# Layer 1 of a two-layer expert kernel: pinned residual additions and weightings, and tiles turned ahead of the products

## Chip, cores and metric

The kernel runs on one core of a Trainium2 chip. The metric is the device time of one execution in microseconds (us). Before the change it is 2111.94 us, the median of three runs. The core has five engines that run side by side, each in its own instruction order: PE (TensorE, the matrix array), DVE (VectorE), ACT (ScalarE), POOL (GpSimd) and SP (SyncE, which only issues transfers here). They wait for each other through semaphores.

## What is computed

A network of two layers on an input of 4 sequences of 512 rows with 512 columns, all in float32. Each layer computes `x = x + attention(layernorm(x)) + experts(layernorm(x))`. The change lies in layer 1, whose two parts are, cut to what matters:

```python
# attention: 16 heads of 32 columns
scores = jnp.einsum('bhqd,bhkd->bhqk', q, k) * scale
attn = jax.nn.softmax(scores, axis=-1)
ctx = jnp.einsum('bhqk,bhkd->bhqd', attn, v)
out = ctx @ wo_w.T + wo_b

# experts: 8 experts, the best 2 for each row
h = jnp.einsum('td,edf->etf', xf, expert_w) + expert_b[:, None, :]
expert_out = jax.nn.silu(h)
combined = jnp.einsum('etf,te->tf', expert_out, full_w.reshape(-1, E))
y = x + combined @ proj_w + proj_b
rms = jnp.sqrt(jnp.mean(y * y, axis=-1, keepdims=True) + EPS)
return norm_w * (y / rms)
```

## The kernel before

Layer 0 fills the time to about 1480 us and is not touched. Layer 1 has 2048 rows, 16 row tiles of 128 rows. Its attention is done in 16 groups g (4 sequences times 4 sets of 4 heads), and each group in 4 places kc, one for each 128 keys. At every place (g, kc) the program records, in this order: the scores of the 4 heads (`weights`, tile `st`, L1114, one matmul a head on a quarter of the array's rows, and the exponential on ACT, L1116, into `pT`), the product with the values of the place before (`attend`, tile `cx`, L1128, with additions on DVE into `pS`, L1134), at some places the key sums (`sum_keys`, `sm`, L1142), inverses (L1152) and scaling of the context (L1160), the next group's queries (`qp`, L1090, with DVE steps L1095 to L1105), the next sequence's values (`vp`, L1050) or a finished tile of the attention's output (`output1`, `o`, L1197). Then `run1((g, kc))` runs the expert jobs that are listed for this place.

These jobs are a list `jobs1` of pairs (place, function); at one place they run in the order of the list. The expert work has two stages.

In the expert stage the rows of x, sorted by expert, are handled in 39 tiles of 128 rows. `fetch_rows`, `fetch_weights` and `fetch_bias` gather a tile's rows, weights and bias by indirect transfers that POOL issues (L384). `turn(i)` transposes the tile on PE (`trm`, L409), and ACT copies the result to `xT` (L411, one buffer). `apply(i)` multiplies (`hp`, L419), adds the bias on DVE into `yr` (L421), takes a tanh on ACT (L425), finishes on DVE (L426) and writes the tile to memory (L427). Tile i is applied at `here = first + 4 + i * 11 // 13`, so about every sixth or seventh place holds two tiles.

In the mixing stage `mix(n)` gathers the two expert results of each row of row tile n (`row0`, `row1`, L434, POOL), loads the tile of normalised x (`xa`, L1222, SP), weights and adds the two results on DVE (L1225, L1226), and adds a bias row on POOL (L1227). One place later `turn_mix` transposes (`trc`, L1234; ACT copy L1238) and brings the partly summed residual tile (`bring`, L1182, SP). `project_mix` multiplies with the projection (`po`, L1245), adds it to `xa` (DVE, L1246), squares and sums on ACT (`ysq`, L1249), and POOL forms the inverse root (`yss`, L1250 and L1251). `finish_mix` scales `xa` by it (DVE, L1256) and calls `add_part`.

`add_part` (L1186) adds one of the two parts, attention or experts, to the residual tile. The second of the two additions is followed by the store to the output (L1189), the first by a store to a scratch array `accd` (L1191) where the tile has to wait in memory. SP issues these stores and loads in its own order.

PSUM holds three banks for the tag "mm", which `hp`, `trm`, `qp`, `vp`, `sm`, `o`, `trc` and `po` take in turn, two double banks for `st` and one for `cx`.

The order of each engine's instructions is not the recorded one: a scheduler in the tile framework reorders them by its own estimates. An instruction that is wrapped in `tc.keep_in_program_order(...)` keeps the place that the program gives it on its engine.

Of the kernel before, what the change touches and what calls it, by code (L numbers as in the profile page):

```python
# [15 lines left out]
ALU = mybir.AluOpType  # L16
# [14 lines left out]
NS = 2 * T // P + E - 1  # L31
# [13 lines left out]
def two_layers(ctx: ExitStack, tc: tile.TileContext, a: dict, out: bass.AP, large: bass.AP):  # L45
# [3 lines left out]
    V, G, A, PE = nc.vector, nc.gpsimd, nc.scalar, nc.tensor  # L49
# [468 lines left out]
    rout = {}  # L518
# [238 lines left out]
    def second_logits(b, pool, bank):  # L757
        def get(rows_):
            V.tensor_tensor(lg1[:, ts(b, TC), :], rows_, rout["rb"].unsqueeze(1).to_broadcast([P, TC, E]), ALU.add)
        return logits(b, rout["rw"], pool, "r1", get, bank)[1]  # L760
# [8 lines left out]
    for b in range(1, B):  # L769
        i = b - 2  # L770
# [46 lines left out]
    at = [(i, h) for i in range(5, len(steps)) for h in range(4)]  # L817
# [5 lines left out]
    at = [(i, h) for i in range(5, len(steps)) for h in (0, 2, 4) if (i, h) > at[2 * NS - 1]]  # L823
# [24 lines left out]
    for n in range(3 * TC):  # L848
        i, t = 29 + n // TC, n % TC
# [13 lines left out]
    qkT, sums_x, first, second, third, fourth, fifth, turn_queries, turn_keys = project(0)  # L863
# [49 lines left out]
    for i, (g, b) in enumerate(steps):  # L913
# [11 lines left out]
        if more:  # L925
            load_sums(i + 1)
            qkT, sums_x, first, second, third, fourth, fifth, turn_queries, turn_keys = project(i + 1)
# [255 lines left out]

    def add_part(n, part_, way):
        x = lies.pop((n, way))
        V.tensor_tensor(x, x, part_, ALU.add)  # L1186
        left[n] -= 1
        if left[n] == 0:
            nc.sync.dma_start(out=out_v[n], in_=x)  # L1189
        elif (n, 1 - way) not in lies:  # L1190
            nc.sync.dma_start(out=accd[ts(n, P), :], in_=x)  # L1191

    def output1(b, t):
        n = b * TC + t
        op = bank1("mm", f"o1_{n}")
        for jj in range(NJ):
            PE.matmul(op, lhsT=cT1[b][:, jj, ts(t, P)], rhs=wa["woT"][:, jj, :],  # L1197
                      start=(jj == 0), stop=(jj == NJ - 1))
        add_part(n, op, 0)

    r1 = Routing("r1", lg1, rp, const, bank1)
# [16 lines left out]
    def mix(n):  # L1218

        g0, g1 = rout["ex1"].gather(n)  # L1220
        x = rout["mix"].tile([P, HID], F32, tag="xr", name=f"xa_{n}")
        nc.sync.dma_start(out=x, in_=xnd[ts(n, P), :])  # L1222

        pin = tc.keep_in_program_order if n < 2 else (lambda x: x)
        pin(V.tensor_scalar(g0, g0, r1.gate[:, 0, n : n + 1], None, ALU.mult))  # L1225
        V.scalar_tensor_tensor(g0, g1, r1.gate[:, 1, n : n + 1], g0, ALU.mult, ALU.add)  # L1226
        G.tensor_tensor(x, x, rows["pb"], ALU.add)  # L1227
        held[n] = g0, x
# [25 lines left out]
    def finish_mix(n):  # L1254
        y, ss = held.pop(n)
        V.scalar_tensor_tensor(y, y, ss[:, 0:1], rows["nw1"], ALU.mult, ALU.mult)  # L1256
        add_part(n, y, 1)


    at = [(g, kc) for g in range(NG) for kc in range(TC)]  # L1260
    jobs1 = [(at[0], lambda: second_logits(B - 1, rp, bank1)()), (at[1], r1.choose), (at[3], r1.place)]
# [5 lines left out]
    first = 9  # L1267
# [3 lines left out]
        jobs1.append((at[first], lambda i=i: rout["ex1"].fetch_weights(i)))  # L1271
        jobs1.append((at[first], lambda i=i: rout["ex1"].fetch_bias(i)))
    jobs1.append((at[first], lambda: rout["ex1"].fetch_weights(2)))
    for i in range(NS):

        here = first + 4 + i * 11 // 13
        jobs1.append((at[here - 1], lambda i=i: rout["ex1"].turn(i)))
        jobs1.append((at[here - 1], lambda i=i: rout["ex1"].fetch_rows(i + 2)))
        jobs1.append((at[here], lambda i=i: rout["ex1"].apply(i)))
        jobs1.append((at[here], lambda i=i: rout["ex1"].fetch_weights(i + 3)))  # L1280
        jobs1.append((at[here], lambda i=i: rout["ex1"].fetch_bias(i + 2)))
    first += 6 + NS * 11 // 13
    jobs1.append((at[first], begin_mixing))
    for n in range(NT):
        here = first + n * 13 // 16
        for d, f in ((0, mix), (1, turn_mix), (2, project_mix), (3, finish_mix)):
            jobs1.append((at[here + d], lambda n=n, f=f: f(n)))
# [78 lines left out]
    for t in range(TC):  # L1366
        PE.matmul(last[t], lhsT=cT1[B - 1][:, NJ - 1, ts(t, P)], rhs=wa["woT"][:, NJ - 1, :], start=False, stop=True)
        add_part(n0 + t, last[t], 0)
        if t == 0:
            fine = bank1("mm", "fine")  # L1370
            PE.matmul(fine[0:1, 0:1], lhsT=ends[:, 0, 0:1], rhs=ones[:, 0:1], start=True, stop=True)
            few = small.tile([1, 1], F32, tag="few", name="few")
            V.tensor_scalar(few, fine[0:1, 0:1], P - 0.5, None, ALU.is_lt)
            V.tensor_tensor(large, few, wide, ALU.max)
# [686 lines left out]
```

## Time and profile before

| what | value |
|---|---|
| time, median of 3 runs | 2111.94 us (2111.6 to 2112.5) |
| the profiled execution | 2114.76 us |
| its span | 2112.8 us |
| mean granted TensorE clock | 0.996 |
| busy: PE, DVE, ACT, POOL | 2057.1, 1463.7, 872.0, 732.8 us |
| L419, the products of the expert tiles, both layers | 520 matmuls, 235.0 us |
| waits of DVE at L1256 (`xa`) for POOL at L1251 (`yss`) | 29.7 us in 14 times |
| layer 1's expert stage | from the first transposes at 1583.84 us to about 1945 us |
| layer 1's mixing stage | about 1948 to 2091 us |

The span is the time between the first and the last instruction in the trace; the time of an execution is a little longer. Times of single instructions come from one profiled execution and are counted from the start of its span. A row of the timeline gives the start, the duration, the engine, the line, the operation, its output and inputs, and how many like instructions it stands for; a bracket behind it tells how long the engine was idle before it and which instruction ended that. Matmuls overlap at their ends, so differences of starts are used for what a group takes.

### The profile page before, as it was taken

How to read it: one execution, taken by the hardware profiler on the slowest of the kernel's cores; microseconds unless marked ns; L12 is line 12 of the kernel's file. 1: busy time of each engine (PE TensorE's matmuls, PEld its weight loads, DVE VectorE, ACT ScalarE, POOL GpSimd, SP SyncE). 2: the span in 40 equal slices, each digit the busy share in tenths (PEclk: the TensorE clock that was granted, in tenths of full speed). 3: DMA queues.
4: the chain of work that ended last, by engine and by line, in shares of the span. 5: the costliest groups of instructions: out<-in, count | busy, mean ns of one | idle time of the engine just before them, and what ended most of it. 6: DMA issues, size and time to landing. Idle time of an engine off the chain costs nothing.

```text
span 2112.8 us, 27908 instructions
## 1 busy us (share of the span) xinstructions
PE 2057.1 (97%) x9138; PEld 1229.1 (58%) x9138; DVE 1463.7 (69%) x3514; ACT 872.0 (41%) x2661; POOL 732.8 (35%) x722
## 2 busy tenths in 40 slices
PE   7999999999999999999999999999999999999988
PEld 4566666666666666666666666665334445445443
DVE  7978967666766766666676778787486555556775
ACT  3444544444444444444443444444243332333332
POOL 3322244443323333333332344453113432332650
PEclk9999999999999999999999999999999999999999
DMA  7201123323332333343233222221316775673551
GB/s 251 76 31 58 39 97 114 143 100 110 126 127 95 121 136 100 110 141 111 95 134 129 76 70 71 70 90 61 115 57 220 258 239 181 217 239 122 143 167 56
DMA packets 95818, 258.73 MB, mean 122 GB/s; under 512 B 12913, under 2 KB 25201, under 8 KB 85681
## 3 DMA queue, kind: packets, MB, share of 16 engines
q0 software_dynamic: 25712, 139.48, 20.0%
q1 hardware_dynamic: 68800, 115.29, 16.4%
q10 hardware_dynamic: 1152, 2.10, 0.3%
q8 instruction: 75, 1.23, 0.2%
q14 instruction: 79, 0.64, 0.1%
HBM read 212.52 MB, written 44.30 MB: 122 GB/s over the span
## 4 chain that ended last, share of the span: by engine, by line
PE 78%; DVE 9%; issue 4%; ACT 4%; POOL 3%; DMA 2%; SPq 0%; ACTq 0%; POOLq 0%; DVEq 0%
PE p L555 22%; PE hp_r L419 13%; PE op L722 10%; PE st L647 4%; PE qp L1090 3%; PE st L1114 3%; PE sp L638 2%; PE cx L1128 2%; PE trm_r L409 2%; PE o L1197 2%; ACT sq L459 2%; PE ca L691 2%; PE vp L1050 1%; PE trq L575 1%; PE trs L673 1%
## 5 line engine op out<-in xcount | busy, mean ns | idle before, releaser
L722 PE MATMUL op<-Wo,cT 128*128 128x512 f32 x512 | 230.4, 598 | 4.9 <-DVE lv L619 3.1
L419 PE MATMUL hp_r<-we_r,xT_r 128*128 128x512 f32 x520 | 235.0, 595 | 0.0
L655 POOL TENSOR_TENSOR lT<-lT,lmask 128x512 f32<-128x512 f32 (+1 forms) x128 | 156.4, 1234 | 182.5 <-ACT lT L651 182.3
L384 POOL DMA_INDIRECT xr_r<-xnd,rows_r x78 | 101.1, 1296 | 293.0 <-PE trm_r L409 243.9
L555 PE MATMUL p<-wB,x 128*128 128x384 f32 x512 | 176.4, 488 | 4.1 <-DVE u L611 3.4
L555 PE MATMUL p<-wT,x 128*128 128x384 f32 x512 | 179.5, 493 | 0.7 <-DVE wT L106 0.7
L555 PE MATMUL p<-wA,xnT 128*128 128x384 f32 x512 | 173.3, 489 | 0.4 <-DVE u L590 0.4
L722 PEld LDWEIGHTS op<-Wo,cT 128*128 128x128 f32 x512 | 92.0, 190 | 114.6 <-issue 77.2
L459 ACT ACTIVATE sq<-qb 128x128 f32<-128x128 f32 x384 | 119.0, 310 | 89.9 <-DVE qb L604 35.3
L419 PEld LDWEIGHTS hp_r<-we_r,xT_r 128*128 128x128 f32 x520 | 94.8, 190 | 104.5 <-issue 96.0
L1116 ACT ACTIVATE pT<-st 128x1024 f32<-128x1024 f32 x128 | 123.9, 1018 | 68.4 <-PE st L1114 57.4
L725 DVE TENSOR_TENSOR acc<-acc,op 128x512 f32<-128x512 f32 x128 | 87.7, 685 | 72.3 <-PE op L722 72.0
L555 PEld LDWEIGHTS p<-wB,x 128*128 128x128 f32 x512 | 94.0, 190 | 67.5 <-issue 9.6
L555 PEld LDWEIGHTS p<-wT,x 128*128 128x128 f32 x512 | 95.2, 193 | 63.3 <-issue 8.9
L555 PEld LDWEIGHTS p<-wA,xnT 128*128 128x128 f32 x512 | 95.0, 192 | 59.8 <-DVE u L590 1.6
L411 ACT COPY xT_r<-trm_r 128x512 f32<-128x512 f32 x78 | 45.3, 581 | 203.4 <-PE trm_r L409 168.0
L569 ACT ACTIVATE qb<-qb,ss 128x128 f32<-128x128 f32 x256 | 81.9, 390 | 111.6 <-POOL ss L461 108.5
L651 ACT ACTIVATE lT<-st,ss 128x256 f32<-128x256 f32 (+1 forms) x128 | 46.8, 448 | 177.8 <-PE st L647 177.7
L647 PE MATMUL st<-qkT 128*128 128x256 f32 (+1 forms) x512 | 109.3, 354 | 0.0
L434 POOL DMA_INDIRECT row_r<-yd,slot_r x64 | 74.8, 1169 | 96.2 <-DVE row_r L1226 35.5
L647 PEld LDWEIGHTS st<-qkT 128*128 128x128 f32 x512 | 92.0, 191 | 10.9 <-issue 1.0
L461 POOL TENSOR_TENSOR ss<-ss,nhalf 128x6 f32<-128x6 f32 x64 | 95.2, 1488 | 5.3
(320 smaller groups left out, 4334.3 us busy)
## 6 DMA issues: line engine op xcount, KB each, us to landing
x<-xsd SPq DMA_DIRECT2D x112, 256.0 KB
yd<-yr_r SPq DMA_DIRECT2D x78, 256.0 KB
wA<-in_wA SPq DMA_DIRECT2D x16, 384.0 KB
wB<-in_wB SPq DMA_DIRECT2D x16, 384.0 KB
xnd<-xn SPq DMA_DIRECT2D x24, 256.0 KB
accd<-acc SPq DMA_DIRECT2D x18, 256.0 KB
acc<-in_x SPq DMA_DIRECT2D x16, 256.0 KB
Wo<-in_Wo SPq DMA_DIRECT2D x8, 512.0 KB
```

Source lines behind the costliest of these rows:

```text
L384: G.indirect_dma_start(out=out, out_offset=None, in_=src, in_offset=at_rows(idx[:, i : i + 1]))
L419: PE.matmul(hp, lhsT=xT[:, k, :], rhs=w[:, ts(k, HID)], start=(k == 0), stop=(k == KC - 1))
L434: G.indirect_dma_start(out=x, out_offset=None, in_=self.yd, in_offset=at_rows(self.r.slot[:, k, n : n + 1]))
L459: A.activation(sq, x[:, h, :], AF.Square, accum_out=ss[:, h : h + 1])
L461: G.tensor_tensor(ss, ss, nhalf[:, 0:n], ALU.pow)
L555: PE.matmul(p, lhsT=x[:, k, ts(c, P)], rhs=w[:, k, :], start=(k == 0), stop=(k == 1))
L569: A.activation(x[:, j, :], x[:, j, :], AF.Copy, scale=sq[t][:, j : j + 1])
L647: PE.matmul(st[:, ds((t % 2) * 256, n)], lhsT=qkT[:, HG + h, ts(t, P)], rhs=qkT[:, h, ds(t * P, n)], start=True, stop=True)
L655: G.tensor_tensor(dst, dst, lmask.rearrange("p a w j -> p (a w j)")[:, 0:n], ALU.mult)
L722: PE.matmul(op, lhsT=cT[:, h, ts(t, P)], rhs=wo[:, h, :], start=(h == 0), stop=(h == HG - 1))
L725: V.tensor_tensor(acc[:, n, :], acc[:, n, :], op, ALU.add)
L1116: A.activation(pt[:, ts(pair, 2), :], st, AF.Exp, scale=SCALE1)
```

## The change

Three edits. The addition in `add_part` is kept in program order for all tiles. The first of the two weightings in `mix` is kept in program order for all row tiles, where it was so for the first two. In the expert stage the jobs for turning a tile and for fetching the rows of the next but one now stand in the list ahead of all products, so at one place they run before them; and of two tiles that are applied at the same place, only the first is turned one place earlier, the second at that place itself.

```diff
     def add_part(n, part_, way):
         x = lies.pop((n, way))
-        V.tensor_tensor(x, x, part_, ALU.add)
+        tc.keep_in_program_order(V.tensor_tensor(x, x, part_, ALU.add))
         left[n] -= 1
...
-        pin = tc.keep_in_program_order if n < 2 else (lambda x: x)
-        pin(V.tensor_scalar(g0, g0, r1.gate[:, 0, n : n + 1], None, ALU.mult))
+        tc.keep_in_program_order(V.tensor_scalar(g0, g0, r1.gate[:, 0, n : n + 1], None, ALU.mult))
         V.scalar_tensor_tensor(g0, g1, r1.gate[:, 1, n : n + 1], g0, ALU.mult, ALU.add)
...
-    for i in range(NS):
-
-        here = first + 4 + i * 11 // 13
-        jobs1.append((at[here - 1], lambda i=i: rout["ex1"].turn(i)))
-        jobs1.append((at[here - 1], lambda i=i: rout["ex1"].fetch_rows(i + 2)))
+
+    here_ = [first + 4 + i * 11 // 13 for i in range(NS)]
+    turned_at = [h - (i == 0 or here_[i - 1] < h) for i, h in enumerate(here_)]
+    for i, h in enumerate(turned_at):
+        jobs1.append((at[h], lambda i=i: rout["ex1"].turn(i)))
+        jobs1.append((at[h], lambda i=i: rout["ex1"].fetch_rows(i + 2)))
+    for i, here in enumerate(here_):
         jobs1.append((at[here], lambda i=i: rout["ex1"].apply(i)))
         jobs1.append((at[here], lambda i=i: rout["ex1"].fetch_weights(i + 3)))
         jobs1.append((at[here], lambda i=i: rout["ex1"].fetch_bias(i + 2)))
```

Nothing else is added or removed: the instructions are the same, in another order.

## The prediction

> **What bounds the kernel now.** The profile's page comes first, for the engine that sets the end.
>
> ```profile
> PE 2057.1 (97%) x9138; PEld 1229.1 (58%) x9138; DVE 1463.7 (69%) x3514; ACT 872.0 (41%) x2661; POOL 732.8 (35%) x722
> PE   7999999999999999999999999999999999999988
> PEclk9999999999999999999999999999999999999999
> ```
>
> PE is busy for 97% of the span, so the kernel is bound by TensorE's own work and order, and the change adds no matmul. What it can move is where PE breaks off a group, where it waits, and the last two slices, where it reads 8. The change lies behind 1580 us. The timeline of PE there is next (start, duration, engine, line, operation, count, idle time before):
>
> ```profile
> 1691.81 3.60 PE L419 MATMUL hp_r<-we_r,xT_r 128*128 128x512 f32 x8
> 1695.34 1.12 PE L1114 MATMUL st<-qk 32*128 32x512 f32 x2
> 1696.39 3.70 PE L419 MATMUL hp_r<-acc,xT_r 128*128 128x512 f32 x8
> 1699.93 0.60 PE L409 MATMUL trm_r<-ident,xr_r 128*128 128x128 f32 x4
> 1700.46 1.13 PE L1114 MATMUL st<-qk 32*128 32x512 f32 x6
> ...
> 1706.07 3.60 PE L419 MATMUL hp_r<-we_r,xT_r 128*128 128x512 f32 x8
> 1709.50 0.60 PE L409 MATMUL trm_r<-ident,xr_r 128*128 128x128 f32 x4
> 1710.03 1.14 PE L1114 MATMUL st<-qk 32*128 32x512 f32 x8
> ```
>
> Two records are one head of scores, eight are the four heads of a place. From start to start a piece of one head takes 1.05 us (1695.34 to 1696.39), three heads 1.06, four 1.07 (to 1711.10). A piece has one price, however many heads it holds. No bracket stands on these rows: PE has no idle time here. Idle PE rows are few, and three are large:
>
> ```profile
> 1803.82 0.60 PE L409 MATMUL trm_r<-ident,xr_r 128*128 128x128 f32 x4
> 1806.43 0.63 PE L409 MATMUL trm_r<-ident,xr_r 128*128 128x128 f32 x4 [2.01 <-DVE yr_r L426]
> ...
> 2013.40 1.99 PE L1090 MATMUL qp<-xnT,wqT 128*128 128x256 f32 x8 [1.95 <-DVE xnT L1186]
> ...
> 2056.92 5.37 PE L1245 MATMUL po<-pw,combT 128*128 128x512 f32 x8 [2.37 <-DVE acc L1186]
> ```
>
> The first lies in the expert stage, the other two in the mixing stage, behind an addition to the residual. The releaser named in the first row is not the true one: the transpose needs only its rows, which POOL issued at 1800.62, behind weights (1798.12) and bias (1799.36), and 5.8 us from issue to 1806.4 fits a landing. The clock by windows shows what followed, the column behind the five busy shares:
>
> ```profile
> 1808.00:1809.00 1.00, 1.00 (x8) 0.20 (x8) 0.00 (x0) 0.66 (x1) 0.95 (x1) 0.50 1.13 418
> ...
> 1810.00:1811.00 1.00, 1.00 (x5) 0.50 (x2) 1.00 (x2) 0.28 (x1) 0.00 (x0) 0.50 1.03 389
> ```
>
> Last come the waits of DVE, for the mixing stage (total, times, longest):
>
> ```profile
> DVE xa L1256 <- POOL yss L1251: 29.7, 14, 3.9
> ```
>
> **The change part by part.** The sum is made against the profiled execution, 2114.76 us (span 2112.8 and 1.96 around it), 2.82 above the median of 2111.94; I carry the difference over to the median.
>
> *Cut score groups: +10.0.* I lay the order of instructions of both programs side by side. With the turns ahead of the applies, tile i+1's transposes stand ahead of tile i's product. The scheduler then sends the product in between the heads of a score group in more places: 45 pieces of scores in this stage become 53. The eight new cuts are in groups 4, 5, 6, 8, 9 and 10 at kc=2, each now transpose, one head, product, three heads, and one more piece each in 6 and 10 at kc=1. Before, such a place takes product 3.43, transposes 0.53, scores 1.07: 5.03. After, transposes 0.53, one head 1.05, product 3.63 (from 1742.52 to 1746.15, between two score pieces), rest 1.06: 6.27. That is 1.25 each, 8 x 1.25 = 10.0. PE is gap-free here, so nothing hides it, and a gain is excluded; the floor is 8 x 1.05 = 8.4. In the other places the exchange of transposes and product is neutral if a transpose group before a full-array product takes 0.44, as layer 0 shows (912.32 to 912.76). If it costs 0.10 more in its 24 places, 2.4 are added, so the ceiling is 12.4. I take 10.0, as the layer 0 row is the same pair of instructions.
>
> The Trainium skill's "TensorEngine Tiling (Array Packing)", Key Properties, speaks against this change too: a change of tiling mode drains TensorE. The rows price that at about 0.10 a switch, which is in the 3.63 above; the page gives no figure.
>
> *PSUM banks: +0.6.* A turned tile in front of the product takes one of the three "mm" banks earlier. Behind sm, qp, qp the product would find its bank held: the DVE reader L1103 ends at 1707.07, and PE would arrive at 1706.07 + 0.44 = 1706.5. That is 0.57 a time, and the inserted head (1.05) covers it in all those places, which is what the cuts are there for. One place has no cover, the product of tile 26, behind o1_3 and two turned tiles (0.96): DVE's addition L1186 of an o1 ended 1.5 behind its last matmul in group 5 (1721.77, 1723.32), so 0.6 remain. Bounds 0 and 1.2.
>
> *Tile 27: -3.8.* Tile 27 is the second of its pair, is turned a place later, and its rows are issued ahead of weights and bias. Before, the stretch from its pair's first transposes to the next product took 10.37 us (1803.82 to 1814.19); the same pieces without a wait took 6.6 at 1857.17. The difference is 2.0 of waiting and 1.8 of a clock at 0.50. What is late next is tile 28, the new pair's second: issued behind tile 26's transposes, its rows have product 3.6, scores 1.1, context 1.0, o1 3.5 and transposes 0.4, 9.6 us, for a landing that took 5.8. So nothing is late. Bounds -3.8 and -2.0.
>
> The Trainium skill, "TensorE: Matmul & The Clock Gate", Part 1, ties the half clock to an idle window of about 3.4 us that runs free. This trace shows 0.50 after 2.01 and 2.37 us of waiting, and 1.00 after 1.95, so short waits can suffice. By the page's rule the wait would not be the cause, this term would be -2.0 and the sum 1.8 higher.
>
> *Start: -1.75.* Tile 1's transposes wait 1.56 for their rows at 1586.00. Moved a place on, the stretch 1583.84 to 1586.56 shrinks to 0.53 (-2.19), and 0.44 comes back later. Bounds -2.2 and 0, if tile 2's rows, issued at 1586.0, are late instead.
>
> *Mixing stage (1948 to 2091): -3.0.* PE's order is unchanged here; DVE's is not. Before, weightings stood between two additions to pS, ahead of the addition that frees the next product: at 2008.32 to 2012.67 DVE does L1225, pS, L1226 (1.75 beside POOL's work), pS, and only then L1186, for which PE waits 1.95. After, the weighting pair (0.40 + 0.75) stands between L1246 and L1256, in the wait for yss (29.7 us in 14 times), the pS pair together, then L1186. PE loses 14.5 us in the stage, 9.5 before 2062 (5.2 in small waits, 2.45 at 2056.92 and 1.7 of slow clock behind it). If only PE counted, 9.5 would go. But the row at 2047.65 in the chain of waits shows what is late next: SP writes accd (4.50), brings the next (3.40), writes out (4.61), loads xa (2.89), POOL adds the bias, and only then L1256 at 2068.02. That chain starts from earlier finishes (L1256 at 2046.15), and it moves by what DVE gains there: worked place by place, 3.0 at the addition of tile 10. POOL's order moves too: gathers of the second row now stand behind yss, since their buffers come free with the later weighting; SP brings one tile ahead of a load. Bounds -9.5 and 0.
>
> *End: -0.4.* SP reads the flag (0.53) and computes on it (0.2 and issue time) ahead of the last three stores instead of behind the last, where it ended at 2107.7. If the end waits on SP, 0.9 go, if it waits for the last store's landing, none. I take about half.
>
> Sum: 10.0 + 0.6 - 3.8 - 1.75 - 3.0 - 0.4 = +1.65. Profiled 2116.4; on the median 2113.6.
>
> **The rivals.** *Mixing all PE (faster).* If SP's chain has slack, the mixing stage gives 9.5, not 3.0: -4.85, 2107.1. For it: PE's large waits there name L1186 by itself. Against it: the chain of waits runs through SP from 2047 to 2065, not through PE.
>
> *The weighting waits for its row (slower).* The first weighting is now pinned on DVE in front of L1256, so the finish, its addition, the pS pair and the o1 addition queue behind it, and PE behind those. Place: the ten or so tiles with that order. It decides where a gathered row lands later than about 0.9 us behind L1246, since yss takes some 2.1 and the pair 1.2. L1225 waited 3.3 us for rows in 6 times before, 0.55 each; ten of them are 5.5, and the gain of 3.0 is gone: +10.15, 2122.1. Against it: POOL's gather of such a row stands one tile's yss earlier, 8.0 us in the rows 2016.42 and 2024.42, where a landing takes 3.75.
>
> *The rows stay late (the change does not do what it says).* If the DMA queues and not POOL's order made tile 27 late, the wait and its slow clock reappear at tile 28: +5.45, 2117.4. For it: DMA shares of 0.96 to 1.13 around 1808. Against it: 9.6 us of lead.
>
> **How the numbers follow.** Forecast 0.60, mixing all PE 0.14, waiting weighting 0.12, late rows 0.14. A measurement of this kernel can tell about 0.2%, 4.2 us, from no change: faster is below 2107.7, slower above 2116.2. Faster: the 0.14 and 0.03 of the forecast's low side, 0.17. Slower: 0.12, 0.14 and 0.05 of the forecast's high side (cuts at 12.4), less 0.02 where these meet a better mixing, 0.29. Same: 0.54. The range reaches from the all-PE case, 2106.5, to 2118.5, past the late rows, and leaves out the waiting weighting and little else.
>
> **What would show it.** Right: score pieces of 1.05 between transposes and product at six kc=2 places; no idle row and a full clock around tiles 27 and 28; tile 1 without its 1.56; no 1.95 at the products behind o1_8; L1256's waits for yss about halved. Wrong: the stretch from the first transposes to 1945 shorter by more than 1 us (my sum there is +5), or idle PE rows in front of hp_r, which would make the bank term the large one; a mixing stage that is shorter by over 6 or longer; L1225 with DMA waits of several us.

## The result, and the profile after

The changed kernel takes 2120.99 us (median of 6 runs, 2119.47 to 2122.72), the kernel before 2112.03 beside it. The ratio is 1.004, its 95% interval 1.003 to 1.005: slower by some 9 us. The forecast was 2113.6 with a range up to 2118.5, so the time lies outside it.

The first row of the page of the changed kernel:

```profile
PE 2064.4 (97%) x9138; PEld 1228.0 (58%) x9138; DVE 1468.0 (69%) x3514; ACT 873.7 (41%) x2661; POOL 730.7 (34%) x722
```

PE is busy for 7.3 us more with the same 9138 matmuls: groups that are cut take longer, and so does work at a low clock. In the second edit two lines became one, so a line of the mixing stage has a number lower by one in the rows of the changed kernel: L1227, L1251 and L1256 are L1226, L1250 and L1255 there.

To place the difference I compare the starts of the same PE groups in two traces, counted from the first transposes of layer 1, so that layer 0, which both kernels share, is out of it (it was 2.1 us shorter in this profiled execution). "Expert stage" is the shift gained up to the attention output tile at 1932.94 us of before, "mixing stage" from there to the first matmul of L1367 at 2101.58. A plus is a longer stage.

| kernel | median, us | expert stage | mixing stage |
|---|---|---|---|
| the change | 2120.99 | +4.1 | +2.7 |
| turns_only | 2119.84 | +4.4 | +0.1 |
| weightings_only | 2116.54 | +2.0 | +2.4 |
| adds_only | 2113.20 | -1.3 | -0.4 |
| second_later | 2105.84 | -8.0 | -0.3 |
| turns_whole | 2110.58 | -5.3 | +3.4 |
| later_whole | 2105.77 | -9.5 | +1.9 |
| before_no_bias | 2105.93 | -0.1 | -7.5 |
| weightings_no_bias | 2102.88 | -1.5 | -10.0 |
| weightings_one_row | 2111.62 | +0.3 | -1.1 |
| weightings_late_bias | 2107.71 | 0.0 | -6.2 |
| later_late_bias | 2105.55 | -8.0 | -0.8 |
| later_weightings_late_bias | 2099.83 | -8.0 | -6.2 |

The kernel before ran beside all of them, with medians of 2112.0 to 2113.6. In the expert stage a kernel that does not touch it still differs by up to 2 us, because the waits of tiles 1 and 27, and the slow clock behind them, are not the same in each execution. In the mixing stage slow clock is counted too: a stretch at 0.50 takes 3.41 us and costs 1.7. The kernel before has one such stretch there, the changed kernel and weightings_only have three, and the kernels whose bias addition is left out or moved have none.

In the changed kernel the remaining 0.8 us of the 7.5 that the two traces differ by after the first transposes lie behind L1367 (its new number is L1368).

**The expert stage, as forecast.** PE's timeline, a cut group and the stretch of tiles 27 and 28:

```profile
1625.55 0.60 PE L409 MATMUL trm_r<-ident,xr_r 128*128 128x128 f32 x4
1626.08 1.12 PE L1114 MATMUL st<-qk 32*128 32x512 f32 x2
1627.13 3.70 PE L419 MATMUL hp_r<-acc,xT_r 128*128 128x512 f32 x8
1630.76 1.13 PE L1114 MATMUL st<-qk 32*128 32x512 f32 x6
1631.83 1.06 PE L1128 MATMUL cx<-pT,v 128*32 128x512 f32 x8
...
1808.39 3.70 PE L1197 MATMUL o<-woT,cT 128*128 128x512 f32 x8
1811.93 1.04 PE L409 MATMUL trm_r<-ident,xr_r 128*128 128x128 f32 x8
1812.87 3.70 PE L419 MATMUL hp_r<-acc,xT_r 128*128 128x512 f32 x8
```

From 1625.55 to 1631.83 are 6.28 us for transposes, one head, product and three heads, where the forecast had 6.27. Tiles 27 and 28 are transposed together without a bracket: the wait is gone and did not come back, and neither did tile 1's.

**The mixing stage, against the forecast.** POOL's timeline, then the DVE and PE rows that follow from it:

```profile
2026.44 1.26 POOL L1226 TENSOR_TENSOR xa<-xa,pb 128x512 f32<-128x512 f32 x1 [4.51 <-DMA xa<-xnd]
2027.86 0.97 POOL L434 DMA_INDIRECT row_r<-yd,slot_r  x1 [0.16 <-PE qp L1090]
2029.17 0.56 POOL L1250 TENSOR_TENSOR yss<-yss,nhalf 128x1 f32<-128x1 f32 x1
```

```profile
2029.77 0.75 DVE L1255 SCALAR_TENSOR_TENSOR xa<-xa,yss,nw 128x512 f32<-128x512 f32 x1 [5.04 <-POOL yss L1250]
2031.39 0.49 DVE L1224 TENSOR_SCALAR row_r<-row_r,gate_r 128x512 f32<-128x512 f32 x1
```

```profile
2035.77 1.17 PE L1233 MATMUL trc<-ident,row_r 128*128 128x128 f32 x8 [3.75 <-DVE qk L1103]
```

POOL stands 4.51 us at the bias addition of tile 9, whose xa is still being loaded. Behind it in POOL's queue are the gather of tile 11's first row and the yss of tile 8, though neither has to do with that load. So yss comes at 2029.7, L1255 has waited 5.04 for it, the weighting of tile 11 starts behind it at 2031.39, 0.09 after its row, gathered as late, has landed, and pS, the reciprocals and qk (L1103), which frees the bank for the next transposes, follow one another on DVE. PE pays 3.75 us and, by the clock column behind the five shares, a slow clock:

```profile
2037.00:2038.00 1.00, 1.00 (x8) 0.38 (x8) 1.00 (x2) 0.63 (x2) 1.00 (x1) 0.50 0.76 213
```

The order of these instructions on POOL is not new. In the kernel before, too, the gather and yss stood behind the addition of tile 9, but that did not wait, since its load, issued at 2018.52, had landed:

```profile
2021.70 1.26 POOL L1227 TENSOR_TENSOR xa<-xa,pb 128x512 f32<-128x512 f32 x1
```

In the changed kernel the load is issued at 2021.80 and lands 4.2 us later.

PE makes this loss good again. Counted from the output tile, its product of L1244 at 2072.96 comes 138.03 us into the stage, where it came after 138.78 before: its waits for two additions (L1186), 1.95 and 2.37 before, are 1.06 and 0.16. The finishes do not catch up: that of tile 8 comes 2.8 us later into the stage than before, that of tile 13, behind one more load that POOL waits for, 2.7. The end of the stage hangs on them, row by row in the changed kernel, and in the last line the same scores before:

```profile
2070.47 1.27 POOL L1226 TENSOR_TENSOR xa<-xa,pb 128x512 f32<-128x512 f32 x1 [5.88 <-DMA xa<-xnd]
2072.68 0.75 DVE L1255 SCALAR_TENSOR_TENSOR xa<-xa,yss,nw 128x512 f32<-128x512 f32 x1 [4.24 <-POOL yss L1250]
2080.44 2.99 PE L1114 MATMUL st<-qk 32*128 32x512 f32 x8 [3.78 <-ACT pT L1116]
2075.77 2.04 PE L1114 MATMUL st<-qk 32*128 32x512 f32 x8 [0.36 <-ACT pT L1116]
```

ACT's exponential, which frees these scores' banks, stands behind the square of tile 14 on ACT (ysq, 2078.75), and that has waited for DVE's addition of tile 14, which stands behind tile 13's finish. So the 2.7 us of the stage are those of the chain of finishes, and the wait at tile 9 shows where it fell behind.

The waits of POOL and DVE over the stage (total, times, longest) in the changed kernel:

```profile
POOL xa L1226 <- DMA xa<-xnd: 23.3, 9, 5.9
POOL xa L1226 <- DVE row_r L1225: 8.2, 2, 4.7
```

```profile
DVE xa L1255 <- POOL yss L1250: 28.1, 13, 5.0
DVE row_r L1224 <- DMA row_r<-yd,slot_r: 0.6, 2, 0.5
```

Before, POOL waited 14.5 us in 5 times for these loads; now it is 23.3 in 9. DVE's wait for yss, 29.7 before, is not halved. The 8.2 in the second row is put down to DVE's weighting, but the loads landed within 0.1 us of it, at 1972.60 and 1982.23, so these two waits lasted as long for the loads; the addition has no other input than the load and a constant row.

### The profile page after: what moved, and what is told of

Its sections match the earlier page's. It is cut to its first block, busy times and chain, and to the rows that moved or that the text cites. A ratio compares the mean times of both kernels' runs of the same rounds, so it can differ in the third digit from the quotient of the medians.

```text
span 2118.2 us, 27911 instructions
## 1 busy us (share of the span) xinstructions
PE 2064.4 (97%) x9138; PEld 1228.0 (58%) x9138; DVE 1468.0 (69%) x3514; ACT 873.7 (41%) x2661; POOL 730.7 (34%) x722
## 4 chain that ended last, share of the span: by engine, by line
PE 81%; DVE 8%; ACT 3%; POOL 3%; DMA 2%; issue 2%; SPq 0%; ACTq 0%; DVEq 0%; POOLq 0%
PE p L555 21%; PE hp_r L419 13%; PE op L722 10%; PE st L647 4%; PE st L1114 4%; PE qp L1090 3%; PE cx L1128 3%; PE sp L638 2%; PE o L1197 2%; PE trm_r L409 2%; PE ca L691 2%; ACT sq L459 1%; PE qp L1074 1%; PE vp L1050 1%; PE trq L575 1%
## 5 line engine op out<-in xcount | busy, mean ns | idle before, releaser
L384 POOL DMA_INDIRECT xr_r<-xnd,rows_r x78 | 95.6, 1226 | 375.9 <-PE trm_r L409 336.3
L1114 PE MATMUL st<-qk 32*128 32x512 f32 x512 | 96.8, 653 | 3.9 <-ACT pT L1116 3.9
```

Source lines behind the costliest of these rows:

```text
L384: G.indirect_dma_start(out=out, out_offset=None, in_=src, in_offset=at_rows(idx[:, i : i + 1]))
L1114: PE.matmul(st[:, i, :], lhsT=qk[g][rows_, 1, ts(kc, P)], rhs=qk[g][rows_, 0, :], start=True, stop=True)
```

## The experiments

**Each edit by itself.** turns_only has the third hunk of the diff, weightings_only the second, adds_only the first.

> Only the third edit: turns and row fetches ahead of the products, the second tile of a pair turned a place later; additions and weightings as before. Theory A (each edit has its own loss): the expert stage costs 4.1 us, as the two traces show from the first transposes to the mixing stage, and the mixing stage runs as before: about 2116 us against 2112 before, with idle PE rows in the mixing stage as before (1.95 at the queries behind L1186). Rival B (the mixing stage loses because it is entered with another timing, not because of the pins): the whole 9 us appear here, about 2121.

Measured: 2119.84 us, ratio 1.0032 (1.002 to 1.0044). The expert stage is 4.4 longer, the mixing stage 0.1, with the 1.95 at the queries as before. The trace holds theory A; the median's 6.5 over the kernel before stands above the 4.5 of the two stages, and both fit the interval (4.2 to 9.3), so its size is not told apart finely.

> Only the second edit: the first weighting of every row tile is kept in program order. Theory A: POOL's bias addition waits longer for the load of xa, and with it the next gather and yss, so the mixing stage is 3 to 5 us longer: 2115 to 2117, with PE waiting for L1103 (some 1.8 and 3.7 us) and POOL's waits for the load of xa at 20 us or more where before had 14.5. The prediction's own step (weightings in the wait for yss give 3 back): 2109. Rival B: no change, 2112.

Measured: 2116.54, ratio 1.0013 (1.0004 to 1.0022); mixing stage +2.4, PE waiting 1.63 and 3.49 us for L1103 and 2.81 for ACT's exponential at 2078.59, POOL 22.1 us for the loads. Theory A.

> Only the first edit: the addition to the residual is kept in program order. The order of the instructions differs from before at the end alone. Theory A: the last stretch, from the first of the last matmuls L1367 to the end, is 0.8 us longer, as between the two traces: 2112.8. The prediction's step (SP's read of the flag ahead of the last stores is hidden or saves a little): 2111.6. With additions that only matter through the weightings, 2112.0.

Measured: 2113.20, ratio 1.0001 (0.9992 to 1.001). The time alone says nothing, as 0.8 is inside the interval. The trace shows a new wait. DVE and PE rows of the end in the changed kernel:

```profile
2109.33 1.28 DVE L1186 TENSOR_TENSOR acc<-acc,o 128x512 f32<-128x512 f32 x2 [1.11 <-PE o L1368]
2110.67 1.13 PE L1368 MATMUL o<-woT,cT 128*128 128x512 f32 x2 [1.38 <-DVE acc L1186]
```

The same 1.11 and 1.38 stand in adds_only, and in none of the kernels without the first edit. PE multiplies the last four tiles in the order 0, 2, 1, 3. Before, DVE added in PE's order; pinned, it adds 0, 1, 2, 3, so it waits for tile 1, and PE's last product, whose double bank still holds tile 2, waits for DVE. The last store is issued 1.45 us later for it, and the stretch from the first matmul of L1367 to the end is 0.8 longer in both kernels. What the edit costs is not settled by that: the stretch is 0.9 longer in turns_only too and 0.7 in turns_whole, neither of which has the edit, and there the last store is not late.

**Which part of the turns.**

```diff
+    for i, here in enumerate(here_):
+        jobs1.append((at[turned_at[i]], lambda i=i: rout["ex1"].turn(i)))
+        jobs1.append((at[turned_at[i]], lambda i=i: rout["ex1"].fetch_rows(i + 2)))
+        jobs1.append((at[here], lambda i=i: rout["ex1"].apply(i)))
...
```

> Part of the third edit: the second tile of a pair is turned a place later and its rows are fetched there, but each turn stands behind the product of the tile before, as in the kernel before. It has 43 pieces of scores in the expert stage, where before has 45 and the changed kernel 53. Theory A (the cuts are the loss of the expert stage, the later second tile is a gain): tile 27's wait with its slow clock (3.8) and tile 1's (1.75) go, two pieces of 1.05 fewer: 2112 - 7.6 = 2104.4. Rival (the wait moves on to tile 28, and tile 1's to tile 2): 2110 to 2112.

Measured: 2105.84, ratio 0.9968 (0.9956 to 0.998): faster by 0.3%. The expert stage is 8.0 shorter. PE's timeline at tiles 27 and 28:

```profile
1808.24 0.60 PE L409 MATMUL trm_r<-ident,xr_r 128*128 128x128 f32 x4
1808.77 1.12 PE L1114 MATMUL st<-qk 32*128 32x512 f32 x2
1809.82 3.70 PE L419 MATMUL hp_r<-we_r,xT_r 128*128 128x512 f32 x8
1813.36 0.60 PE L409 MATMUL trm_r<-ident,xr_r 128*128 128x128 f32 x4
```

No wait, and the turn stands behind the product. So of the third edit the later second tile gains 8, and the turns ahead of the products take 12 back. turns_only has ten pieces of scores more than second_later, so 12.4 us are 1.24 for each.

**Whole groups of heads.** turns_whole and later_whole keep the matmuls of scores and context in program order:

```diff
-                PE.matmul(st[:, i, :], ...)
+                tc.keep_in_program_order(PE.matmul(st[:, i, :], ...))
...
-            PE.matmul(acc_cx[g][ds(h * D1, D1), :], ...)
+            tc.keep_in_program_order(PE.matmul(acc_cx[g][ds(h * D1, D1), :], ...))
```

> The third edit, with the matmuls of the scores and of the context kept in program order, so that no group of four heads is cut: 37 pieces of scores in the expert stage, where the third edit alone has 53. Theory A (each cut costs 1.05 to 1.25 us, and a PSUM bank that is still held costs some 0.57 in eight places behind sm, qp, qp, and a second product of a pair waits some 0.8 for ACT's copy in six): the expert stage is 16 x 1.1 = 17.6 shorter less 4.6 and 4.8, about 8 shorter than with the third edit alone: +4.4 becomes -4, and 2108 in all. Rival B (the banks come free in time, nothing waits): 12 to 17 shorter, 2100 to 2104. Rival C (a cut costs little, the loss is elsewhere): 2115 or more.

Measured: 2110.58, ratio 0.9987 (0.9977 to 0.9996). The expert stage is 9.7 shorter than with turns_only, between theory A and B: what the cuts had been put in to avoid costs less than they do. PE's timeline, behind sm, qp, qp and at a pair:

```profile
1626.71 0.60 PE L409 MATMUL trm_r<-ident,xr_r 128*128 128x128 f32 x4
1627.42 3.70 PE L419 MATMUL hp_r<-acc,xT_r 128*128 128x512 f32 x8
...
1638.38 3.70 PE L419 MATMUL hp_r<-we_r,xT_r 128*128 128x512 f32 x8 [0.73 <-ACT xT_r L411]
```

The transposes take 0.71 to the product's start instead of 0.44: the held bank costs 0.27, not the 0.57 that the forecast had, and in turns_only a head of 1.05 stands in front of it. The second product of a pair waits 0.73 for ACT's copy. The pins also reach the mixing stage, whose order they change, and it loses 3.4; so the median says less than the expert stage's own number.

> The second tile of a pair turned a place later, each turn behind the product before it (the kernel second_later), and no group of heads cut: 37 pieces where second_later has 43. Each of the six removed cuts gives 1.05, and the second product of a pair then waits for ACT's copy of its transposed rows, 0.6 to 0.8 each by ACT's 0.58 and the way through the semaphores: 6 x 1.05 - 6 x 0.7 = 2 less than second_later, about 2104. If the copies come later, the same as second_later or up to 3 longer.

Measured: 2105.77, the same as second_later. The expert stage is 1.5 shorter (2 expected, with the same waits of 0.73), and the mixing stage gives it back, as it did in turns_whole.

**POOL's queue.** before_no_bias and weightings_no_bias leave out one line of `mix`:

```diff
-        G.tensor_tensor(x, x, rows["pb"], ALU.add)
```

> The kernel before with POOL's addition of the bias row to xa (L1227) left out, so the projection's bias is not added. POOL no longer waits for the load of xa; DVE's L1246 reads the load itself. A control for the next kernel: its mixing stage, from the first trc to the last o of L1367, is the number to compare with; from before's trace that stretch is 154.9 us. All theories: 1 to 8 us shorter than before, as the yss waits shrink by the bias additions ahead of them.

> The kernel with the second edit alone (first weighting kept in program order), and POOL's addition of the bias left out as in the control. Theory A (the loss of the mixing stage arises in POOL's queue: the bias addition waits for the load of xa, and the next row gather and yss stand behind it): with that addition gone the 2.4 us of loss are gone too, and the mixing stage is as long as the control's or up to 3 us shorter, as the prediction had it. Rival B (DVE's own order, or the gathers that are issued behind yss, make the loss): still 2 us or more longer than the control.

Measured: 2105.93 for the control (mixing stage -7.5) and 2102.88 (-10.0). With the addition in POOL's queue the pinned weighting loses 2.4; without the addition it gains 2.5 (3.05 by the medians). Theory A holds, B falls: DVE's new order is good, and the loss needs the addition in POOL's queue.

**The same, with nothing left out.** The addition moves to `turn_mix`, at its end, and is pinned; on POOL it then stands behind the next gather and the yss of the tile before:

```diff
     def mix(n):
-        G.tensor_tensor(x, x, rows["pb"], ALU.add)
...
     def turn_mix(n):
         ...
+        tc.keep_in_program_order(G.tensor_tensor(x, x, rows["pb"], ALU.add))
         held[n] = cT_, x
```

> The second edit alone, and POOL's addition of the bias to xa is recorded in turn_mix (one place later) and kept in program order, so on POOL it stands behind the next row gather and the yss of the tile before, no longer ahead of them. Nothing is left out. Theory A (the pinned weighting loses because gather and yss stand behind a bias addition that waits for its load): the loss of the second edit, 2.4 us in the traces, turns into a gain of 2 to 7: 2105 to 2110. Rival B (the load itself is late and what needs xa is the end of the chain, wherever POOL adds): 2114 to 2117 as with the second edit alone.

Measured: 2107.71, ratio 0.9971 (0.9962 to 0.9981), mixing stage -6.2. The second edit by itself was slower than before; with this line moved it is faster. POOL's timeline and DVE's wait in it:

```profile
2012.99 0.56 POOL L1250 TENSOR_TENSOR yss<-yss,nhalf 128x1 f32<-128x1 f32 x1
2013.53 1.26 POOL L1237 TENSOR_TENSOR xa<-xa,pb 128x512 f32<-128x512 f32 x1
```

```profile
DVE xa L1255 <- POOL yss L1250: 13.9, 15, 1.8
```

The addition comes behind yss and finds its load landed; DVE's waits for yss fall from 31.5 in weightings_only to 13.9, the halving that the forecast had wanted to see.

> The kernel second_later (second tile of a pair a place later, turns behind the products; 2105.8 measured) with the bias addition behind gather and yss as in the kernel above; no weighting pinned. Theory A: 2 to 6 less than second_later, 2100 to 2104 (with the addition left out altogether it was 7). Rival B: 2105 to 2107.

Measured: 2105.55, ratio 0.9962 (0.9948 to 0.9975). Beside second_later's 2105.84 this is no gain that shows (mixing stage -0.8 against -0.3), so theory A was wrong here: without the pinned weightings POOL's order alone is worth next to nothing, since PE still waits 1.95 and 2.04 us for the additions (L1186) that stand behind the weightings on DVE.

> second_later, the later bias addition, and the second edit (first weighting kept in program order). Theory A: the pinned weightings gain here what the prediction gave them, about 2.5 as they did without the bias addition: 2097.5 to 2102. Rival B (pinned weightings lose 2.4 in any order of POOL): 2.4 more than later_late_bias.

Measured: 2099.83 us (2098.46 to 2100.17), ratio 0.9934 (0.992 to 0.9947). This is the fastest, 0.7% below the kernel before and 1% below the changed one. The pinned weightings gain 5.3 in the mixing stage over later_late_bias, twice what was expected. With second_later, later_late_bias and this kernel the two edits stand crossed: moving the addition alone gains 0.5 in the mixing stage, and it turns what the pinned weightings do there from +2.4, as measured in weightings_only, into -5.3.

**Why the load is late.** weightings_one_row takes half of the gathers out of the mixing stage:

```diff
-            for k in range(2):
+            for k in range(1 if self.silu else 2):
...
-        g0, g1 = rout["ex1"].gather(n)
+        g0 = rout["ex1"].gather(n)[0]
+        g1 = g0
```

> The second edit alone with the gather of the second expert's row left out in the mixing stage (the first row is used twice, so half of the rows' traffic is gone). Theory C (the load of xa is late because the second row's gather now starts right behind yss, beside SP's load and store, and the transfers share the DMA engines): POOL's waits for the load of xa fall from some 31 us to 16 or less, and the mixing stage's loss of 2.4 is gone: 2112 or less. Theory D (the load is late because it is issued late, by SP's order and the end of the chain): the waits stay above 20 us, and the time at 2115 to 2117.

Measured: 2111.62, ratio 0.999 (0.9981 to 0.9999), mixing stage -1.1. The time went as theory C said, but its waits did not: POOL waited 48.0 us for the loads, with less else to do. The time that the loads themselves took tells more: the issues between 1955 and 2065 us, with the median from issue to landing last, in turns_only, weightings_only and weightings_one_row:

```profile
xa<-xnd SPq DMA_DIRECT2D x12, 256.0 KB, 3.1
xa<-xnd SPq DMA_DIRECT2D x12, 256.0 KB, 4.1
xa<-xnd SPq DMA_DIRECT2D x13, 256.0 KB, 3.3
```

second_later has 3.1 too. From SP's output store to the bring that waits for it, issue to issue, the picture is the same: 3.7 us on average in the kernel before, 4.5 in the changed kernel and in weightings_only, 3.8 in weightings_one_row. So loads and stores take about 1 us longer where the pinned weightings have moved the gathers, and hardly longer where half of the gathers are gone. That speaks for theory C's cause. Theory D may have a part in it, as SP has one bring ahead of the load of tile 3. With half of the gathers gone the whole stage is lighter, and no such kernel without the second edit was run, so the parts are not told apart. A late load alone costs little: in weightings_late_bias the loads take 4.0 as well, and the stage gains 6.2.

## Why the prediction was wrong, by its own steps

*Cut score groups, +10.0: right.* The price of 1.25 each is in the rows to 0.01 us, and ten pieces between second_later and turns_only cost 1.24 each. Of it 1.05 is the additional piece and 0.20 the two mode switches. The drain at a change of tiling mode, which the Trainium skill's "TensorEngine Tiling (Array Packing)", Key Properties, names, can then be no more than these 0.20. Keeping all groups whole gave 9.7 back, which is net of the waits that it opens.

*PSUM banks, +0.6: too large.* The bank term measured 0.27 where 0.57 was worked out, and at tile 26's product, 1811.93 to 1812.87, there is no wait at all. DVE's addition ended at 1812.81, 0.88 behind the output tile's last matmul, where the group I had read it from had 1.5: there DVE was still busy with pS, here it was idle.

*Tile 27, -3.8, and the start, -1.75: right.* second_later, where only these two and two pieces fewer count, gave 8.0 against 7.6. Part of it is luck: the slow clock behind tile 27's wait, 1.7, stands in the trace that the sum was made against, and adds_only waited 1.92 there and kept a clock of 1.00. The stage as a whole came to +4.1 and +4.4 where the terms add up to +5.05. The rival of rows that stay late is out.

*Mixing stage, -3.0: the step that failed.* It had two halves. That the weightings would fit into the wait for yss was right: weightings_no_bias shows a gain of 2.5 from them, and weightings_late_bias more. That the chain of loads and finishes and not PE sets the end of the stage was right too, as PE's 0.75 of lead at 2072.96 shows. That the chain "moves by what DVE gains there" was wrong, because I followed the chain through SP and DVE and priced POOL only by durations. POOL has one queue, and the chain of the forecast itself had "POOL adds the bias, and only then L1256": I read that as an addition of 1.3 us and not as a place in the queue where a gather and a yss of other tiles stand behind a load, and I took the load at its old 2.9 us, where loads take 4.1 beside the moved gathers. The measured value is +2.7 (+2.4 in weightings_only), the time by which the chain falls behind, and the bounds of the term, -9.5 and 0, ruled out any loss without a reason for it. This term alone, mis-sized by 5.7, puts the time outside the range. The 14.5 us that I gave as PE's loss in the stage are also more than the trace has: 8.5 of idle time from 1948 to 2091 and 1.7 of slow clock.

*End, -0.4: not there.* The stretch is 0.8 longer in the two kernels with the first edit, though not every part of that is the edit's, as said above. I looked at SP's order and not at DVE's, which makes PE wait.

*The slower rival* had the right time, 2122.1, and the right place, the pinned weighting in front of the finish, but the wrong cause. L1224 waited only 0.6 us for its rows; the finish waited for yss. That the time came out so close is luck.

## What to carry to other kernels

An instruction that waits for a transfer holds up everything behind it on its engine, so the place of a small addition in a queue can be worth more than its time: here, beside pinned weightings, a 1.3 us addition that was moved behind two instructions of other tiles turned a loss of 2.4 us into a gain of 6.2. When a change reorders one engine, list what it frees and what that makes the other engines' queues look like, and give a term a bound on the other side unless a row excludes it. A scheduler's filler is not free: it put 1.05 us of broken-off work in front of a wait of 0.27.

## What the runs showed of the hardware

The granted TensorE clock does not follow from the length of a wait alone in these traces. At the same queries, with the same wait of 1.95 us, the kernel before kept a clock of 1.00 and went on in 1.99; turns_only did not, as PE's timeline and the clock column show:

```profile
2018.31 2.59 PE L1090 MATMUL qp<-xnT,wqT 128*128 128x256 f32 x8 [1.95 <-DVE xnT L1186]
```

```profile
2020.00:2021.00 1.00, 1.00 (x4) 0.82 (x3) 0.00 (x0) 1.00 (x2) 0.96 (x1) 0.50 0.40 115
```

The clock stays at 0.50 for 3.41 us, from 2019.58, and costs 1.7 us, as it does in adds_only. Elsewhere a wait of 1.80 us (weightings_only, tile 1) was followed by such a stretch, and one of 2.05 (later_whole, before L1245 at 2047.53) was not. The Trainium skill, "TensorE: Matmul & The Clock Gate", Part 1, has an idle window of about 3.4 us that runs free of the kernel. Two outcomes of one wait would fit a window that runs free, but half clocks behind waits of 1.95 us do not fit one that has to be idle throughout; no run here shows which part differs. For the working of a sum, a wait of about 2 us is to be priced at 2 or at 3.7 us, by chance.
